# A graph network kernel's first edge layer: finer node ranges per column, sums in seven slots a block, a small PSUM bank in two halves

## The chip, the cores and the metric

The kernel runs on one core of a Trainium2 chip. The metric is the device time of one execution in microseconds. The kernel has TensorE (PE; its weight loads are listed apart as PEld), VectorE (DVE), ScalarE (ACT), GpSimd (POOL) and SyncE (SP), which fetch their own instruction streams and meet at semaphores. DMA queues are fed by SP, ACT and POOL.

## What is computed

The reference has four stages over 6250 nodes with 256 features: a message passing layer over 106250 edges, a graph attention layer that chooses among four experts, a second message passing layer, and a second mixture of experts. The change touches the first one only:

```python
h = jnp.concatenate([x[row], edge_attr], axis=1)      # x: layer norm of the nodes
h = jax.nn.relu(h @ W1 + b1)
agg = jax.ops.segment_sum(h, col, num_segments=N_NODES)
cnt = jax.ops.segment_sum(jnp.ones((h.shape[0],), h.dtype), col, num_segments=N_NODES)
agg = agg / jnp.maximum(cnt, 1.0)[:, None]
out = jnp.concatenate([x, agg], axis=1)
return jax.nn.relu(out @ W2 + b2)                     # added to the nodes
```

The edges come sorted by their target node.

## The kernel before

**Blocks and groups.** The nodes are cut into 49 blocks of 128 (the last one has 106). The edges that end in a block lie in one window of 18 columns of 128 edges. A column index is written as a range `k` of three columns (six ranges) and a place `t` in it. A group is the work of 6 columns, the ranges `g` and `g + 3`; three groups make a block, and the stage runs over 147 groups. The product with the node part of `W1` is made beforehand and lies in memory as `y_dram`.

**One turn of the loop.** For group q the loop writes, engine by engine in an order that `Ordered.pin` keeps:

- `join(q-1)`: DVE adds the gathered rows to the products of the edge features (L1518), ACT applies the relu (L1519). The rows lie in a ring of four buffers `h`.
- `hidden(q, 0)`, `hidden(q, 2)`, `hidden(q, 4)`: PE multiplies the turned edge features `et` by `w1b` into `ph` (L1115), eight matmul records in each of the three. An instruction in f32 stands as two records in the trace.
- `add_up(q-2)`: PE sums the rows by node (L1541), with a 0/1 matrix `eq` as weights. Since the edges are sorted, a range reaches only some of the four quarters (32 nodes) of the block, which `QUARTERS` lists. For each column and quarter there is one matmul on a 128 by 32 tile of the array. In groups 0, 1 and 2 of a block these are 12, 12 and 9 matmuls; in the last block all are full 128 by 128 ones (L1533).
- `load_sources(q+2)`: POOL gathers six columns of rows of `y_dram` by index, one indirect DMA for each (L1128). They may overwrite the ring buffer that `add_up(q-2)` read.
- `turn(q+1)`: DVE turns the next edge features (L1500, tile `et`); `equal(q)`: DVE makes `eq` (L1225), with three buffers `eq`, and one buffer `eq4` for the last block.
- `load_attr(q+4)`: SP and ACT issue the edge features' loads (L1410).

**Work in between.** Three times a turn `steps` moves small jobs on by one step: a sort for the attention layer (DVE), the index windows of later blocks (`load_windows`, with two PE transposes and a count), and `end_of(w)`, the end of a block: division by the count, a transpose (L1109), the product with `W2`, layer norm, another transpose, and a product with `wgx`. A job waits between its hops by `yield`. All of these share one PSUM tile `pt` (pool `p1`, one buffer): who asks for it next waits until its last reader is done. The sort ends in `sorted_edges`, which transposes five pieces, copies each to `lt` (two buffers, L1335) and writes it to memory (L1336).

After the stage the first experts' products (L1115 with `ph<-b_all,w`) and the attention layer follow; they take over the PSUM of `ph`.

Of the kernel before, what the change touches and what calls it, by code (L numbers as in the profile page):

```python
# [1 line left out]

# [19 lines left out]
def spread(n):  # L22

    cuts = [n] if n % 16 == 0 else [n // 16 * 16, n]
    return list(zip([0, *cuts[:-1]], cuts))


class Ordered:
# [840 lines left out]
def kernel(ctx: ExitStack, tc: tile.TileContext, a: dict, out: bass.AP):  # L869
# [32 lines left out]
    NR = CW // NT  # L902
    Q = P // 4
    QUARTERS = ((0, 1), (0, 2), (1, 3), (1, 4), (2, 4), (3, 4))
    H, X = a["L0_ffn_att_src"].shape
    HX = H * X
    GW = HX + 2 * H
# [36 lines left out]
    with ExitStack() as fast:  # L944
# [188 lines left out]
        def load_windows(b, pool):  # L1133

            sl = slice(b * TB, (b + 1) * TB)
            n = TB * CW

            def flat3(v):
                return v.rearrange("p w a t -> p w (a t)")

            raw = {k: wix.tile([P, P], I32, name=f"raw_{k}") for k in ("src", "dst")}
            for w in range(b * TB, (b + 1) * TB):
                at, r = (w - b * TB) * CW, start_of(w)
                for k, v in raw.items():
                    rows = a[k][bass.ds(r, WE)].rearrange("(j p) -> j p", p=P)
                    SY.dma_start(v[at : at + CW, :], rows)  # L1146
            for _ in range(3):
                yield

            def turned(k):  # L1150

                pt = pool.tile([P, D], F32, name="pt")[:, 0:n]
                TE.transpose(pt, whole[k][0:n, :], ident[0:n, 0:n])
                return pt

            whole = {}
            for k, v in raw.items():
                whole[k] = v.bitcast(F32)
                V.tensor_copy(whole[k][0:n, :], v[0:n, :])
            yield  # L1160
            pt = turned("src")
            g = wix.tile([P, n], F32, name="ix_g")
            V.tensor_scalar(g, pt, 0.0, float(N), op0=OP.is_lt, op1=OP.mult)
            V.tensor_add(g, g, pt)
            V.tensor_scalar(
                src1[:, sl, :, :].rearrange("p w a t -> p (w a t)"), g, 0.0, float(N - 1),
                op0=OP.max, op1=OP.min,
            )
            yield
            V.scalar_tensor_tensor(  # L1170
                flat3(dst1[:, sl, :, :]), turned("dst").rearrange("p (w k) -> p w k", k=CW),
                float(-b * TB * P), base.unsqueeze(2).to_broadcast([P, TB, CW]),
                op0=OP.add, op1=OP.subtract,
            )
            yield
            inside = wix.tile([P, TB, NR, NT], F32, name="inside")
            d = dst1[:, sl, :, :]
            V.tensor_scalar(flat3(inside), flat3(d), 0.0, None, op0=OP.is_ge)
            V.scalar_tensor_tensor(
                flat3(inside), flat3(d), P - 0.5, flat3(inside), op0=OP.is_lt, op1=OP.mult  # L1180
            )

            n = TB - (b == NB - 1)
            for k, (lo, hi) in enumerate(QUARTERS):
                for limit, op in ((lo * Q - 0.5, OP.is_gt), (hi * Q - 0.5, OP.is_lt)):
                    if 0 < limit < P - 1:
                        V.scalar_tensor_tensor(
                            inside[:, :n, k, :], d[:, :n, k, :], limit, inside[:, :n, k, :],
                            op0=op, op1=OP.mult,
                        )  # L1190
            if n < TB:
                V.scalar_tensor_tensor(
                    inside[:, n, :, :], d[:, n, :, :], LAST - 0.5, inside[:, n, :, :],
                    op0=OP.is_lt, op1=OP.mult,
                )
            V.tensor_reduce(good[:, b : b + 1], flat3(inside), axis=AX.XY, op=OP.add)
# [14 lines left out]
        def equal(pool, w, q):  # L1211


            total = NT * Q * sum(hi - lo for lo, hi in (quarters(w, q), quarters(w, q + NG)))
            if w < T - 1:
                eq = pool.tile([P, EQ], F32, name="eq", bufs=3)
            else:
                eq = pool.tile([P, total], F32, name="eq4", bufs=1)
            found, at = {}, 0
            for k in (q, q + NG):  # L1220
                lo, hi = quarters(w, k)
                n = (hi - lo) * Q
                found[k] = eq[:, at : at + NT * n].rearrange("p (t n) -> p t n", n=n)
                at += NT * n
                V.tensor_tensor(  # L1225
                    found[k], lane[:, None, lo * Q : hi * Q].to_broadcast([P, NT, n]),
                    dst1[:, w, k, :].unsqueeze(2).to_broadcast([P, NT, n]), op=OP.is_equal,
                )
            return found
# [88 lines left out]
        def sorted_edges(pst, wk):  # L1318
# [10 lines left out]
                V.tensor_scalar(some, some, -1.0, 127.0, op0=OP.mult, op1=OP.add)  # L1329
                V.tensor_copy(v, some)  # L1330
            for c in range(KA // P):
                pt = pst.tile([P, 4, P], F32, name="pt")
                TE.transpose(pt[:, 0, :], some[:, c * P : (c + 1) * P], ident)
                lt = wk.tile([P, P], BF16, name="lt")
                SC.activation(lt, pt[:, 0, :], AF.Copy)  # L1335
                SC.dma_start(low_dram[c * P : (c + 1) * P, :], lt)  # L1336
            V.tensor_reduce(good2[:, 1:2], good3[:, :, 0], axis=AX.X, op=OP.add)
# [17 lines left out]
        with ExitStack() as layer:  # L1355
# [40 lines left out]
                return both  # L1396

            V.memset(gtab[:, :, HX : HX + H], 1.0)
            groups1 = [(w, g) for w in range(T) for g in range(NG)]

            def load_attr(q):

# [66 lines left out]
            with (  # L1469
# [1 line left out]
                tc.tile_pool(name="y0", bufs=1) as wy,  # L1471
                tc.tile_pool(name="ph1", bufs=2, space=PSUM) as psh,
                tc.tile_pool(name="pe1", bufs=1, space=PSUM) as pse,
                tc.tile_pool(name="p1", bufs=1, space=PSUM) as psm,
            ):

                ring = [wy.tile([P, G1, HS], F32, name=f"h{i}") for i in range(4)]
                for h in ring:
                    V.memset(h[:, :, D:WS], 1.0)
                equals, et, ph, sums = {}, {}, {}, {}  # L1480

                last_of = [
                    max(k % NG for k, (lo, hi) in enumerate(QUARTERS) if lo <= b < hi)
                    for b in range(4)
                ]
                NQ1 = len(groups1)

                def rows_of(q):
                    return ring[q % len(ring)]

                def load_sources(q):

                    w, g = groups1[q]
                    for j, (k, t) in enumerate(chunk(g)):
                        gather(rows_of(q)[:, j, 0:D], y_dram, src1[:, w, k, t : t + 1])

                def turn(q):

# [22 lines left out]

                def add_up(q):

                    w, g = groups1[q]
                    if g == 0:
                        sums[w] = pse.tile([P, WS], F32, name="pe")
                    h, eq = rows_of(q), equals.pop(q)

                    for j in reversed(range(NT)):
                        for i, k in ((1, g + NG), (0, g)):  # L1530
                            lo, hi = quarters(w, k)
                            if hi - lo == 4:
                                TE.matmul(  # L1533
                                    sums[w], eq[k][:, j, :], h[:, i * NT + j, 0:WS],
                                    start=g == 0 and j == NT - 1 and i == 1,
                                    stop=g == NG - 1 and j == 0 and i == 0,
                                )
                                continue
                            for b in range(lo, hi):
                                at = slice((b - lo) * Q, (b - lo + 1) * Q)  # L1540
                                TE.matmul(  # L1541
                                    sums[w][b * Q : (b + 1) * Q, :], eq[k][:, j, at],
                                    h[:, i * NT + j, 0:WS], start=g == 0 and j == NT - 1,
                                    stop=g == last_of[b] and j == 0,
                                )

                def end_of(w):

# [3 lines left out]
                    V.reciprocal(rc, rc)  # L1552
                    ag = wk.tile([P, D], F32, name="o")
                    SC.activation(ag, pe[:, 0:D], AF.Copy, scale=rc)
                    yield
                    yield
                    gt = wk.tile([P, D], F32, name="o")
                    transposed(psm, gt, ag)
                    yield
                    yield  # L1560
                    pm = psm.tile([P, D], F32, name="pt")
                    both = (b_all[:, w, 0:P], b_all[:, w, P:D], gt[:, 0:P], gt[:, P:D])
                    mm(pm, lambda c: both[c], lambda c: w2[:, c, :], 4)
# [16 lines left out]
                    V.scalar_tensor_tensor(off, mv[:, 0:1], -1.0, rs, op0=OP.mult, op1=OP.mult)  # L1580
                    xn = wk.tile([P, D], F32, name="o")
                    SC.activation(xn, x_all[:, w, :], AF.Identity, bias=off, scale=rs)
                    yield
                    yield
                    transposed(psm, b_all[:, w, :], xn)
                    yield
                    yield
                    pg = psm.tile([P, D], F32, name="pt")
                    mm(
                        pg[:, 0:GW], lambda c: b_all[:, w, c * P : (c + 1) * P],  # L1590
# [35 lines left out]
                                some.remove(n)  # L1626

                for q in range(3):
                    load_sources(q)
                turn(0)  # L1630
                ordered = Ordered(tc)
                for q in range(NQ1 + 2):
# [5 lines left out]
                    if q >= 2:  # L1638
                        add_up(q - 2)
                        if (q - 2) % NG == NG - 1:  # L1640
                            work.append(end_of((q - 2) // NG))
                    if 3 <= q + 2 < NQ1:
                        load_sources(q + 2)
                    if q + 1 < NQ1:
                        turn(q + 1)
                    if q < NQ1:
# [1012 lines left out]
```

## Time and profile before

| | |
|---|---|
| median of 4 runs | 3422.54 us (3417.98 to 3426.49) |
| profiled execution | 3417.23 us, its span 3415.3 us |
| mean granted TensorE clock | 0.904 |
| PE, PEld busy | 3169.7 us (93%), 2533.0 us (74%) |
| DVE, ACT, POOL busy | 2155.8 us (63%), 1127.0 us (33%), 2248.2 us (66%) |
| first and last gather of the stage start | 93.8 us, 1233.6 us |
| records of the sums L1541 | 3168 |

The profile is one execution. Its times count from the first instruction. "Idle before" is what an engine stood still just before the instructions of a row, and behind it stand those whose end released it. Busy shares over the whole span mix stages with different limits, so the stage of the change has to be read by itself.

### The profile page before, as it was taken

The page shows a single profiled execution, that of the slowest core. Times are in us where ns is not written, and L with a number is a line of the kernel's source. Part 1 is how long each engine was busy: PE and PEld are TensorE (multiplying, and loading weights), DVE is VectorE, ACT ScalarE, POOL GpSimd, SP SyncE. Part 2 cuts the span into 40 slices and gives each one's busy share as a digit, 9 for nine tenths or more (in the row PEclk, how much of TensorE's full clock was granted, in tenths as well). Part 3 has the DMA queues.
Part 4 walks back from the last instruction along what each step waited for, and adds up shares of the span by engine and source line. Part 5 has one row for each costly group of instructions (what it writes and reads, how often), then busy time and mean ns, then how long its engine had stood idle before and what let it go on. Part 6 is the DMA issues. An engine that isn't in the chain of part 4 may idle for free.

```text
span 3415.3 us, 57220 instructions
## 1 busy us (share of the span) xinstructions
PE 3169.7 (93%) x18509; PEld 2533.0 (74%) x18509; DVE 2155.8 (63%) x5685; ACT 1127.0 (33%) x2014; POOL 2248.2 (66%) x2364
## 2 busy tenths in 40 slices
PE   7899999999999989999999999995689988989898
PEld 5677777777777777888888888883556666666677
DVE  5677787767766767877575858775234444445464
ACT  5122222222222224345545455661012212212134
POOL 0677777777777736766555556625777777777773
PEclk9999999999999999999999999996566677677797
DMA  6999999999999943334343434443112222222221
GB/s 195 198 211 205 203 202 205 201 197 208 203 209 207 206 111 105 98 83 137 83 124 97 133 85 126 114 97 88 53 53 60 59 59 60 59 59 66 59 63 37
DMA packets 698912, 428.56 MB, mean 125 GB/s; under 512 B 531272, under 2 KB 640315, under 8 KB 698604
## 3 DMA queue, kind: packets, MB, share of 16 engines
q0 software_dynamic: 89408, 178.08, 23.0%
q1 hardware_dynamic: 365948, 187.21, 21.0%
q10 hardware_dynamic: 243248, 59.52, 9.6%
q8 instruction: 150, 2.46, 0.3%
q14 instruction: 158, 1.29, 0.1%
HBM read 382.05 MB, written 42.49 MB: 124 GB/s over the span
## 4 chain that ended last, share of the span: by engine, by line
PE 64%; POOL 14%; DMA 9%; issue 7%; DVE 3%; ACT 1%; SPq 1%; ACTq 0%; POOLq 0%; DVEq 0%
PE ph L1115 31%; POOL hg L1128 13%; PE py L1115 11%; PE po L1884 6%; PE pe L1541 5%; DMA hg<-hp_dram,src 5%; PE pt L1115 4%; PE pe L2524 2%; DMA rb<-low_dram 2%; PE pa L1821 1%; POOL h L1128 1%; DMA ea<-in_edge_attr_dram 1%; PE pt L1109 1%; PE pm L1115 1%; SPq L1146 0%
## 5 line engine op out<-in xcount | busy, mean ns | idle before, releaser
L1128 POOL DMA_INDIRECT h<-y_dram,src x882 | 844.3, 957 | 388.9 <-issue 263.1
L1128 POOL DMA_INDIRECT hg<-hp_dram,src x831 | 786.7, 947 | 267.7 <-issue 223.9
L1128 POOL DMA_INDIRECT sg<-gat_dram,src x640 | 612.3, 957 | 352.2 <-issue 161.5
L1115 PE MATMUL ph<-w1b,et 128*128 128x256 f32 x3528 | 823.5, 385 | 11.5 <-DVE et L1500 10.0
L1115 PEld LDWEIGHTS ph<-w1b,et 128*128 128x128 f32 x3528 | 655.7, 190 | 154.1 <-issue 70.3
L2524 PE MATMUL pe<-eq,hg 128*128 128x96 f32 (+15 forms) x2036 | 435.1, 350 | 151.3 <-DMA hg<-hp_dram,src 129.1
L2524 PEld LDWEIGHTS pe<-eq,hg 128*128 128x128 f32 x2036 | 382.4, 257 | 256.4 <-issue 98.5
L1519 ACT ACTIVATE h<-h 128x1536 f32<-128x1536 f32 x147 | 218.2, 1485 | 586.6 <-DMA h<-y_dram,src 218.8
L1518 DVE TENSOR_TENSOR h<-ph,h 128x1536 f32<-128x1536 f32 x147 | 258.3, 1757 | 228.4 <-PE ph L1115 202.2
L2503 DVE TENSOR_SCALAR eq<-px,dst,ew 128x96 f32<-128x96 f32 x831 | 261.6, 368 | 219.6 <-PE pe L2524 131.5
L1115 PE MATMUL py<-w,hh 128*128 128x256 f32 x1568 | 385.4, 386 | 4.9 <-ACT hh L1720 4.5
L1115 PE MATMUL ph<-b_all,w 128*128 128x256 f32 (+1 forms) x1600 | 386.7, 381 | 2.9 <-issue 2.8
L1115 PEld LDWEIGHTS py<-w,hh 128*128 128x128 f32 x1568 | 290.4, 192 | 41.5 <-ACT hh L1720 6.7
L1115 PEld LDWEIGHTS ph<-b_all,w 128*128 128x128 f32 x1600 | 291.2, 191 | 36.1 <-issue 3.2
L1500 DVE STREAM_TRANSPOSE et<-ea 128x1536 f32<-128x1536 f32 x147 | 260.9, 1775 | 15.4 <-DMA ea<-in_edge_attr_dram 9.3
L1720 ACT ACTIVATE hh<-ph,b 128x256 f32<-128x256 f32 (+1 forms) x400 | 166.2, 467 | 288.5 <-PE ph L1115 280.8
L1884 PE MATMUL po<-pp,B 128*128 128x240 f32 (+10 forms) x1280 | 252.1, 337 | 2.1 <-DVE acc L1890 2.0
L1884 PEld LDWEIGHTS po<-pp,B 128*128 128x128 f32 x1280 | 215.6, 190 | 14.2 <-DVE acc L1890 2.8
L1541 PE MATMUL pe<-h,eq 128*32 128x257 f32 x3168 | 216.8, 384 | 0.0
L1863 DVE TENSOR_TENSOR pp<-px,A 128x960 f32<-128x960 f32 (+10 forms) x160 | 155.9, 974 | 3.9 <-PE po L1884 3.5
L1541 PEld LDWEIGHTS pe<-h,eq 128*32 128x32 f32 x3168 | 95.9, 109 | 83.5 <-issue 30.5
L1720 ACT ACT_TABLE_LOAD x98 | 125.7, 1283 | 49.8 <-PE ph L1115 48.4
(339 smaller groups left out, 3800.7 us busy)
## 6 DMA issues: line engine op xcount, KB each, us to landing
ea<-in_edge_attr_dram SPq DMA_DIRECT2D x588, 96.0 KB
ea<-in_edge_attr_dram ACTq DMA_DIRECT2D x588, 96.0 KB
y<-y SPq DMA_DIRECT2D x196, 128.0 KB
w<-in_L_ffn_W_dram SPq DMA_DIRECT2D x48, 512.0 KB
y<-ys SPq DMA_DIRECT2D x96, 256.0 KB
rb<-low_dram SPq DMA_DIRECT2D x80, 256.0 KB
h<-y_dram,src POOLq DMA_INDIRECT x882
hg<-hp_dram,src POOLq DMA_INDIRECT x831
```

What stands on the lines that cost most here:

```text
L1109: TE.transpose(pt[:, c, :], src[:, c * P : (c + 1) * P], ident)
L1115: TE.matmul(dst, lhs(c), rhs(c), start=c == 0, stop=c == n - 1)
L1128: GP.indirect_dma_start(out=dst, out_offset=None, in_=table[0:NP, :], in_offset=IndirectOffsetOnAxis(ap=idx, axis=0),)
L1500: V.transpose(et[q].rearrange("p c m k -> p m c k"), ahead.pop(q).rearrange("p i m (c k) -> p (i m) c k", c=2),)
L1518: V.tensor_add(h, ph.pop(q), h)
L1519: SC.activation(h, h, AF.Relu)
L1541: TE.matmul(sums[w][b * Q : (b + 1) * Q, :], eq[k][:, j, at], h[:, i * NT + j, 0:WS], start=g == 0 and j == NT - 1, stop=g == last_of[b] a ...
L1720: SC.activation(hidden[u][:, f, :n, :], ph[:, f - f0, :n, :], AF.Gelu, bias=b1[:, e, f : f + 1],)
L1863: V.tensor_tensor(pps[g, half][:, :, 0:n, :], pay[:, js, :].unsqueeze(2).to_broadcast([P, HG, n, HV]), near[g][:, js, 0:n].unsqueeze(3).to ...
L1884: TE.matmul(po.rearrange("p b v -> p (b v)"), B[:, j, :], pp[:, j, 0:n, :].rearrange("p b v -> p (b v)"), start=half == 0 and j == 0, stop ...
L2503: V.tensor_scalar(equals[k][:, j, :], lanes[:, 0:NW], dst_of[:, t : t + 1], ew[:, t : t + 1], op0=OP.is_equal, op1=OP.mult,)
L2524: TE.matmul(sums[b][:, lo - t0 * P : hi - t0 * P], hg[:, j, :], eq[:, j, lo - n0 : hi - n0], start=False, stop=after >= (t0 + n) * P,)
```

## The change

It has six parts.

- **Ranges for each column.** `RANGES` gives each of the 18 columns its own range of quarters, instead of one for three columns. There are 26 pairs of column and quarter in a block instead of 33. `load_windows` tests whether the edges keep to these ranges, in six instructions over several columns instead of ten over three.
- **Slots.** `planned()` writes the 26 matmuls as slots of up to four, one for each quarter, and gives the three groups of a block 2, 2 and 3 slots. The groups run in the order 2, 0, 1 (`TURNS`). A column that finds no slot in its own group is summed in the next one; only the columns at places 2 and 5 of a group (`LATE1`) may be.
- **Gathers.** The columns of `LATE1` are loaded one turn later, ahead of the next group's other four.
- **`eq`.** Four buffers instead of three; the last block takes two of them for a group instead of the one of its own.
- **The bank.** `pt` becomes one tile of two halves, handed out in turn by `Halves`.
- **Hops.** `end_of` waits three steps instead of two at four places; `lt` has one buffer instead of two.

```diff
+    TURNS, SLOTS = (2, 0, 1), (2, 2, 3)
+    RANGES = (((0, 1), 3), ((0, 2), 2), ((1, 2), 2), ((1, 3), 3), ((2, 3), 1), ((2, 4), 3), ((3, 4), 4))
+    reach = [r for r, n in RANGES for _ in range(n)]
...
+class Halves:
+    def __init__(self, pool, width):
+        self.width, self.last = width, 1
+        self.bank = pool.tile([P, 2, width], F32, name="pt")
+    def tile(self, shape, dtype, name):
...
+            self.last = 1 - self.last
+            v = self.bank[:, self.last, 0:n]
...
-            if w < T - 1:
-                eq = pool.tile([P, EQ], F32, name="eq", bufs=3)
-            else:
-                eq = pool.tile([P, total], F32, name="eq4", bufs=1)
...
+                if eq is None or w == T - 1:
+                    eq, at = pool.tile([P, EQ], F32, name="eq", bufs=4), 0
...
-                lt = wk.tile([P, P], BF16, name="lt")
+                lt = wk.tile([P, P], BF16, name="lt", bufs=1)
...
-            groups1 = [(w, g) for w in range(T) for g in range(NG)]
+            groups1 = [(w, g) for w in range(T) for g in TURNS]
...
+                    for i, g in enumerate(TURNS):
+                        for j, (k, t) in enumerate(chunk(g)):
+                            for b in range(*reach[k * NT + t]):
+                                left[b].append((i, j, k, t))
+                        for n in range(SLOTS[i]):
+                            for b in range(4):
+                                if left[b]:
+                                    plan.append((i, b, *left[b].pop(0)))
...
+                LATE1 = (NT - 1, 2 * NT - 1)
+                EARLY1 = tuple(j for j in range(G1) if j not in LATE1)
...
+                    for i, b, own, j, k, t, start, stop in plan:
+                        if i == turn:
+                            of = q - turn + own
+                            lo = QUARTERS[k][0]
+                            TE.matmul(
+                                sums[w][b * Q : (b + 1) * Q, :],
+                                equals[of][k][:, t, (b - lo) * Q : (b - lo + 1) * Q],
+                                rows_of(of)[:, j, 0:WS], start=start, stop=stop,
+                            )
...
-                    yield
-                    yield
+                    for _ in range(3):
+                        yield
...
+                    if 3 <= q + 1 < NQ1:
+                        load_sources(q + 1, LATE1)
                     if 3 <= q + 2 < NQ1:
-                        load_sources(q + 2)
+                        load_sources(q + 2, EARLY1)
```

## The prediction

> **What bounds the kernel now.** The change lies in the first edge layer, so I cut the span by windows of time first. The two lines below hold the quiet part of the stage (only sums, products and block ends) and the part in which index windows are also made.
>
> ```profile
> 861.00:1230.20 369.20, 369.20 (x2467) 287.76 (x2466) 259.17 (x433) 105.44 (x176) 275.94 (x289) 1.00 0.94 204
> 176.00:860.00 684.00, 671.83 (x4476) 520.25 (x4471) 518.04 (x1005) 189.90 (x319) 501.81 (x525) 1.00 1.03 204
> ```
>
> After the window and its length stand PE, PEld, DVE, ACT and POOL in us, then the granted clock, the DMA share and GB/s. PE is without a gap in the quiet part and lacks 12 us in the other; the clock is full. The chain that ended last says the same, and gives the prices (start, us, what):
>
> ```profile
> 1199.64 1.73 PE ph L1115 x8
> 1201.36 1.44 PE pe L1541 x24
> 1202.80 5.38 PE ph L1115 x24
> 1208.18 0.22 PE pt L1109 x2
> 1208.40 1.43 PE pe L1541 x18
> 1209.83 3.65 PE ph L1115 x16
> ...
> 1231.44 1.43 PE pe L1541 x18
> ```
>
> Everything on it is PE. From 1208.40 to 1231.44 is one block of three groups: 23.05 us. Eight records of 256 columns take 1.73 us, 0.216 each. A sum of 18 records (9 matmuls) takes as long as one of 24 (12 matmuls): four quarters run side by side, and what counts is the number of rounds, not of matmuls. Three slots of two rounds (f32 makes two records) are six rounds.
>
> The second resource to look at is POOL, in the answer for the gathers' line:
>
> ```profile
> L1128 POOL DMA_INDIRECT h<-y_dram,src x882: 940/947/1374, 93.8 to 1233.6; - x177
> L1128 POOLq EVENT_SEMAPHORE  x147: 42/4259/9199, 87.3 to 1220.2; - x147
> ```
>
> In the timeline one gather follows the other with 0.30 us between. From 199.17 to 233.15, 27 steps without a wait take 33.98 us, 1.2585 each; 18 of them are 22.65 us, and a block takes 23.05. So POOL is just behind PE, with 0.4 us a block in hand. That the joins wait for PE and hardly for gathers stands in the costliest groups:
>
> ```profile
> L1518 DVE TENSOR_TENSOR h<-ph,h 128x1536 f32<-128x1536 f32 x147 | 258.3, 1757 | 228.4 <-PE ph L1115 202.2 <-DMA h<-y_dram,src 20.6 <-PE pt L1115 4.7
> ```
>
> Last, the end of the stage. DVE's waits from 1230 to 1262, and the timeline at the copies of `lt`:
>
> ```profile
> DVE eq L1225 <- PE pe L1533: 12.4, 2, 7.1
> ```
> ```profile
> 1263.93 0.28 ACT L1335 ACTIVATE lt<-pt 128x128 bf16<-128x128 f32 x1 [0.87 <-DMA low_dram<-lt]
> 1264.24 0.33 ACTq L1336 DMA_DIRECT2D low_dram<-lt  x1
> ```
>
> The single `eq4` holds DVE until the sums of the group before are done, and the join behind it waits too. The last product of the stage ends at 1245.0, the last join starts at 1251.67, and the experts' first products start at 1253.5, when that join gives their PSUM free.
>
> **The change part by part.**
>
> *Slots (PE).* A block goes from nine slots to 2+2+3. Each slot less is two rounds of 0.216: 0.432 us; two a block are 0.864, and over 48 blocks 41.5 us (the last block keeps its full matmuls). From 33 to 26 matmuls nothing more comes. The step in and out of the 32-wide form is paid once a group as before. A block on PE is then 23.05 - 0.86 = 22.19 us.
>
> *Gathers (POOL).* Their number and bytes stay. With PE at 22.19 and POOL at 22.65 a block, POOL becomes the bound. Its line: first start at 93.8, and 881 steps. At 1.2585 the last one starts at 1202.5 instead of 1233.6, 31.1 us sooner. Bounds: at 0.947 + 0.305 = 1.252 it is 1196.8; at the mean of 957 ns, 1.262, it is 1205.6; should the gathers stretch as much again as the gap of mean over median, 1.272, it is 1214.4. I take the unblocked row. On top, POOL now runs ahead: the gathers of group 144 end 11.0 us before its join (1218.54 to 1229.54). Where POOL was the late one, early in the stage, it was 4.6 us at group 3 (123.7 to 128.3) and 3.15 us at group 6 (146.28 to 149.43). The difference to their mean, 3.9, is 7.1 us; it is taken up once and is a gain too. The transfers' rate must rise by 2%, from 204 GB/s to 208; the window from 800 to 900 us has 208 already.
>
> *Late columns.* Two of six gathers move to the next turn, ahead of the other four, so POOL's stream keeps its order of groups. All six wait for `add_up(q-2)` as before. For the late pair a turn is lost: they end some 2.5 us after that sum and must land before a join some 10 us later; landing at group 6 took less than 3.15. Free.
>
> *Semaphores on POOL.* In the built program the gathers hold 716 semaphore instructions, 573 more. Upper bound: 42 ns each on POOL's line, 24 us. Lower: 0, since today's 147 stand ahead of the first gather of a group and the gap there, unblocked, is the same 0.30 us. That row is the same engine and instruction; I take 0.
>
> *`eq`.* With four buffers the last two `equal` no longer wait for the sums of the group before. The last join moves from 1251.67 towards the end of its product at 1245.0: up to 6.7 us. In the other groups a DVE wait on `eq` does not show (the 12.4 us above are all). Free.
>
> *The bank in halves, and the hops.* PE's waits for `pt` between 90 and 1255 us (rows of `pt` on ACT and DVE) sum to about 14 us. At most these go, and in the part with the index windows they would let PE run nearer to POOL; but POOL is the later one there, so I count 0; the bounds are 0 and what rival 4 makes of it. The steps of `end_of` are the same instructions, and in the quiet part no wait hangs on them. At the end of the stage the block's chain is run without turns in between, so longer hops cost nothing there.
>
> *`lt` with one buffer.* Each of five copies waits for the write of the one before: 0.28 + 0.33 + about 1.45 (the chain has such writes at 1.45 and 1.48) is 2.06 us instead of about 0.93 (four steps from 1262.06 to 1265.77). ACT is free 4.2 to 4.5 us later. Behind it stand the experts' first activations, for which PE waits; but before that PE has the last block's sums (4.3 us). I take +2, bounds 0 and +4.5.
>
> *Window test, DVE.* Six instructions for ten, a few tenths a window: nothing.
>
> [...] The row for the halves is the 14 us of waits, counted at 0. The Trainium skill, "PSUM — Partial Sum Buffer", section "PSUM bank collisions raise a hardware error", asks to guard PSUM by bank and quadrant, not by address; guarded like that the halves would bring nothing, which leaves the sum as it is. The row for the gathers has a mean of 957 ns over a median of 947, so other work costs them 10 ns each, 9 us in all; the same DVE work in 2 to 4% less time adds under 1 us. [...]
>
> **The sum**, against the profiled execution. Last join by POOL: 1202.5 + 0.95 + 3.9 = 1207.4. By PE: 1245.0 - 41.5 = 1203.5. The later counts, 1207.4; it was 1251.67, so -44.3. With `lt` +2: -42.3. What follows is the same list of work on PE, apart from a few instructions at the seam, so it moves as a whole. 3417.23 - 42.3 = 3374.9. The median of the runs lies 5.3 above the profiled run; I keep that: 3380.
>
> **The rivals.**
>
> 1. *POOL pays for the semaphores or stretches.* For it: POOL has little in hand, and nearly each gather now waits for PE too. Against: today's unblocked gap with a semaphore. At 24 us the last join is at 1231, the gain 18: 3404.
> 2. *Slower: the clock.* Once PE waits for gathers it has gaps. Where PE was busy 57 to 73 of 100 us (2300 to 2500), the granted clock was 0.62 and 0.52. For it: that stage also waits for gathers. Against: from 176 to 860 PE lacks 1.8% and the clock is 1.00, and here it would lack 0.46 of 22.65 us, 2%. A us at half clock costs PE half a us, and PE has 4 us in hand (1203.5 against 1207.4): with x us at half clock the time is 3380 + x/2 - 4. From x = 93 it is no gain, from 107 of the 1110 us it is slower by over 0.2%; at 120 it is 3436.
> 3. *The change doesn't bring the rounds.* If the new order of quarters doesn't run side by side, the rounds stay nine slots' worth, and only the end of the stage gains: -6.7 + 2, 3418. Against: the 9 and the 12 matmuls of today take the same 1.43 us.
> 4. *POOL does not bind.* If the gathers step at 1.252 and the waits for `pt` go, the last join is at 1201 and `lt` is hidden: -51, 3372.
>
> **How the numbers follow.** The forecast with its bounds (steps of 1.252 to 1.272, `lt` 0 to 4.5) gives 3372 to 3395, chance 0.65. Rival 4: 0.12. Rival 1: 0.11, 3390 to 3410. Rival 3: 0.04. Rival 2: 0.08, two thirds of it above the old time. Eight in ten: from 3367 (rival 4 less 4 to 5 us, by which the runs scatter about their median) to 3402. A measurement can tell 0.2%, 6.8 us, from no change: faster 0.90, same 0.04, slower 0.06.
>
> **What the profile after would show.** The sums at 1.0 us for the first two groups of a block and 1.43 for the third; 2496 records instead of 3168. A block at 22.6 to 22.7 us in the quiet part, PE with gaps of some tenths, POOL's steps at 1.26 with next to no waits, joins that wait for gathers and no longer for PE. The last gather near 1202. No wait of `eq` for L1533. Wrong would be: steps of POOL above 1.29, sums of 1.43 in all groups, a granted clock under 1 in the stage, or a new wait of PE for `h` or `pt` longer than today's.

## The result: 0.2% slower; the slots' time came back as waits for `pt`

The changed kernel takes 3432.18 us (median of 39 runs, 3417.08 to 3443.91), the kernel before 3423.82 us beside it (62 runs). The ratio is 1.0023, 95% interval 1.0017 to 1.0029. The profiled execution after has a span of 3425.6 us and took 3427.48; before, 3415.3 and 3417.23. The forecast was 3380 us, the range 3367 to 3402.

The slots did what they were meant to do. The group of the sums on the page, and in the timeline the third sum of a block and the three of the next, the last of them cut short by the window's end at 900 us (start, us, engine, line, instruction):

```profile
L1583 PE MATMUL pe<-h,eq 128*32 128x257 f32 x2496 | 175.4, 385 | 0.0
```
```profile
876.93 1.51 PE L1583 MATMUL pe<-h,eq 128*32 128x257 f32 x24
...
883.97 1.07 PE L1583 MATMUL pe<-h,eq 128*32 128x257 f32 x12
...
890.92 1.07 PE L1583 MATMUL pe<-h,eq 128*32 128x257 f32 x16
...
899.03 1.29 PE L1583 MATMUL pe<-h,eq 128*32 128x257 f32 x20
```

2496 records stand where 3168 stood, two-slot sums take 1.07 us and three-slot ones 1.51, the sums' busy time falls from 216.8 to 175.4 us, and the block from 876.93 to 899.03 takes 22.10 us; it was 23.05. Now the same windows of time as before the change, for the part with index windows and for the quiet part:

```profile
176.00:860.00 684.00, 645.04 (x4003) 505.62 (x4003) 509.45 (x987) 183.39 (x312) 489.91 (x512) 0.98 0.95 199
861.00:1230.20 369.20, 364.04 (x2280) 285.22 (x2279) 263.61 (x438) 105.51 (x179) 279.56 (x292) 1.00 1.12 209
```

In the first part PE lacks 39 of 684 us; it lacked 12. From 90 us to the join of group 144 (1229.5 before, 1238.3 after) PE was busy for 1116.5 us before and 1087.9 after, and stood still for 23.0 and 60.4: 28.6 us less work and 37.4 us more standing make the join 8.8 us later. A second pair of profiles (`before_again`, `after_again`) has 37.0 us more standing too, but 38.5 us less work, and there the join comes 1.5 us sooner. So the standing takes back what the slots save, to within a few us. Where the 0.2% come from is not shown: the stage's last join starts 2.9 us later in the first pair and 5.6 us sooner in the second, and behind it the spans go on for 7 and 9 us longer, which is inside the scatter of such stretches (2164 to 2178 us over the profiles of the table below).

PE's waits from 90 to 1250 us say for what (engine, tile and line, what ended the wait: us in all, times, longest):

```profile
PE pt L1136 <- ACT a_dst L1637: 26.1, 8, 8.9
PE pt L1130 <- ACT b_all L1131: 20.3, 9, 8.0
PE ph L1136 <- DVE et L1545: 10.3, 2, 5.8
PE ph L1136 <- DVE rc L1593: 2.1, 4, 0.7
PE pt L1130 <- ACT o L1624: 1.4, 1, 1.4
```

The first two rows are 46.4 us in 17 waits; all waits for `pt` were about 14 us before. L1136 after is L1115 before (products), L1130 is L1109 (transposes), L1564 is L1519 (relu).

The longest one in the timeline. ACTq and SPq are the issues of DMAs; the bracket is the engine's idle time and what ended it:

```profile
623.33 0.28 SPq L1167 DMA_DIRECT2D raw_dst<-in_dst_dram  x1
623.49 0.52 PE L1136 MATMUL pt<-wgx,b_all 128*128 128x24 f32 x4
...
627.66 6.17 ACTq L1434 DMA_DIRECT2D ea<-in_edge_attr_dram  x4
...
631.29 0.28 SPq L1167 DMA_DIRECT2D raw_dst<-in_dst_dram  x1
...
634.10 1.48 ACT L1564 ACTIVATE h<-h 128x1536 f32<-128x1536 f32 x1 [13.42 <-DMA h<-y_dram,src]
635.49 0.17 ACT L1635 ACTIVATE gtab<-pt 128x16 f32<-128x16 f32 x1
...
635.61 0.17 ACT L1637 ACTIVATE a_dst<-pt 128x4 f32<-128x4 f32 x1
635.83 1.36 PEld L1136 LDWEIGHTS pt<-w,b_all 128*128 128x128 f32 x4 [9.30 <-ACT a_dst L1637]
635.83 2.08 PE L1136 MATMUL pt<-w,b_all 128*128 128x256 f32 x4 [8.89 <-ACT a_dst L1637]
```

To be read from the end. PE wants to write the product with `W2` (L1136, `pt<-w,b_all`) and waits 8.89 us for the copy of `a_dst`. That copy reads the *other* product, `pt<-wgx,b_all`, which PE had made at 623.49 into the other half: the halves don't free PE from it, since the wait is one for the whole tile. The copy is late because ACT works in order: ahead of it stands the relu at 634.10, and ahead of that the issue of four edge feature loads from 627.66 to 633.83, while SP issues the raw indices of an index window (619.10 to 631.29). The join that the relu needed had begun at 621.97 already, and ACT had done nothing since 620.67. What held it are waits for semaphores at the loads, not the issues; ACT's instructions at the loads' line from 618 to 636 us (count, shortest/median/longest ns, first and last start):

```profile
L1434 ACTq DMA_DIRECT2D ea<-in_edge_attr_dram x4: 323/341/370, 627.7 to 633.5; - x4
L1434 ACTq EVENT_SEMAPHORE  x2: 38/3390/6742, 620.7 to 620.8; - x2
```

An issue takes 0.34 us; ahead of the first stands a wait of 6.74. In the trace's records each of the four loads uses the semaphore of a `raw_src` load that SP issued before it, waits for that semaphore, and goes out just behind that load's landing: landings at 627.53, 629.09, 630.39 and 633.43, issues at 627.66, 629.11, 630.42 and 633.45. So ACT is held until SP's index loads have landed. In this trace and in those of the kernel before and of `even_c` it is so in all six index windows: 24 of ACT's 588 loads follow a `raw_src` load on their semaphore, all 24 by 0.02 to 0.23 us after its landing.

Where a use of `pt` stands in the block's nine steps (three a turn) follows from the code. With hops of two, a block's end uses `pt` at steps 2 (transpose of `ag`), 4 (product with `W2`), 8 (transpose of `xn`) and 10 (product with `wgx`, step 1 of the next block); with hops of three at 3, 6, 11 and 14, which are 3, 6, 2 and 5 of the nine. So with three, two pairs of uses in a block lie one step apart (2 and 3, 5 and 6), both from a turn's first call of `steps` to its second. Only a sum and eight records of `ph` lie between them on PE, while on ACT the copy between them stands behind the loads issued at the end of the turn before and behind the new turn's relu. With two, one pair is as close (1 and 2), from the third call to the first of the next turn, and its copy is issued ahead of the loads.

Theory H (hold and hops) says that the stall needs both: uses one step apart with a copy of ACT between them, and ACT held by its loads. Rival G: POOL is the bound anyway, and the waits for `pt` only stand where waits for gathers would stand. Rival A: ACT is held whatever the hops are, and the waits move elsewhere.

### The profile page after: what moved, and what is told of

The parts are those of the page before. It is cut to its first block, busy times and chain, and to the rows that moved or that the text cites. A ratio compares the mean times of both kernels' runs of the same rounds, so it can differ in the third digit from the quotient of the medians.

```text
span 3425.6 us, 56495 instructions
## 1 busy us (share of the span) xinstructions
PE 3129.6 (91%) x17837; PEld 2510.1 (73%) x17837; DVE 2156.9 (63%) x5678; ACT 1120.5 (33%) x2013; POOL 2248.7 (66%) x2364
## 4 chain that ended last, share of the span: by engine, by line
PE 53%; DMA 16%; POOL 13%; issue 7%; DVE 6%; ACT 2%; SPq 2%; ACTq 0%; DVEq 0%; POOLq 0%
PE ph L1136 25%; POOL hg L1149 12%; PE py L1136 11%; DMA hg<-hp_dram,src 6%; DMA ea<-in_edge_attr_dram 6%; PE po L1928 5%; PE pt L1136 3%; PE pe L1583 3%; PE pe L2568 2%; DMA h<-y_dram,src 2%; DMA rb<-low_dram 2%; DVE et L1545 1%; PE pa L1865 1%; PE pt L1130 1%; DVE x_all L2109 1%
## 5 line engine op out<-in xcount | busy, mean ns | idle before, releaser
L1136 PE MATMUL ph<-w1b,et 128*128 128x256 f32 x3528 | 830.8, 387 | 12.4 <-DVE et L1545 10.3
L1136 PEld LDWEIGHTS ph<-w1b,et 128*128 128x128 f32 x3528 | 660.7, 192 | 159.1 <-issue 71.3
L1564 ACT ACTIVATE h<-h 128x1536 f32<-128x1536 f32 x147 | 218.3, 1485 | 545.3 <-DMA ea<-in_edge_attr_dram 274.1
L1136 PE MATMUL py<-w,hh 128*128 128x256 f32 x1568 | 384.6, 385 | 5.9 <-ACT hh L1764 5.1
L1136 PE MATMUL ph<-b_all,w 128*128 128x256 f32 (+1 forms) x1600 | 385.3, 380 | 0.3 <-DVE h L1563 0.3
L1136 PEld LDWEIGHTS py<-w,hh 128*128 128x128 f32 x1568 | 289.5, 191 | 42.8 <-ACT hh L1764 7.7
L1136 PEld LDWEIGHTS ph<-b_all,w 128*128 128x128 f32 x1600 | 290.2, 190 | 32.9 <-DVE h L1563 0.7
L1583 PE MATMUL pe<-h,eq 128*32 128x257 f32 x2496 | 175.4, 385 | 0.0
L1136 PE MATMUL py<-ew,g 65*128 65x256 f32 x392 | 132.5, 465 | 0.3 <-ACT g L2488 0.2
```

Source lines behind the costliest of these rows:

```text
L1136: TE.matmul(dst, lhs(c), rhs(c), start=c == 0, stop=c == n - 1)
L1564: SC.activation(h, h, AF.Relu)
L1583: TE.matmul(sums[w][b * Q : (b + 1) * Q, :], equals[of][k][:, t, (b - lo) * Q : (b - lo + 1) * Q], rows_of(of)[:, j, 0:WS], start=start, s ...
```

## The experiments where the kernel before takes 3427 to 3429 us

### Spacing alone, and hold alone

Hops of two again (`hops2_c`), an even spacing (`even_c`: uses at 0, 2, 4 and 6 of the nine), the halves and hops alone on the kernel before (`before_halves_hops3_c`), and ACT's loads given to SP, which takes the reading of their start address from ACT too (`sp_loads_c`):

```diff
 hops2_c, at all four places in end_of
-                    for _ in range(3):
+                    for _ in range(2):
 even_c, at the first, second and fourth place; the third keeps range(3)
-                    for _ in range(3):
+                    for _ in range(2):
...
-                    for _ in range(3):
+                    for _ in range(2):
...
-                    for _ in range(3):
+                    for _ in range(6):
 before_halves_hops3_c, on the kernel before: class Halves, psm = Halves(pends, D), and
-                    yield
-                    yield
+                    for _ in range(3):
+                        yield
 sp_loads_c
-                r = start_of(w, mybir.EngineType.Activation)
+                r = start_of(w)
...
-                        (SY if c < 2 else SC).dma_start(
+                        SY.dma_start(
```

hops2_c:

> The changed kernel with hops of two steps, now where the kernel before takes 3427 us and the changed one 3434. Theory H (the hops): 3385 to 3400 us, PE's waits for `pt` under 20 us. Rival G (the gathers are the bound anyway): 3420 to 3435. Rival A (ACT is held by its issue of loads whatever the hops, and the waits move to other uses of `pt`): 3410 to 3425.

even_c:

> The changed kernel with hops of 2, 2, 3 and 6 steps (uses of `pt` at 0, 2, 4 and 6 of a block's nine steps), where the kernel before takes 3427 us. Theory H: waits for `pt` of 5 to 15 us and 3378 to 3398 us, at or under hops of two. Rival A: 3410 to 3430.

before_halves_hops3_c:

> The kernel before with only the halves and the hops of three steps, where the kernel before takes 3427 us. Theory H: 3445 to 3475 us, waits of PE for `pt` of 40 us or more. Rival G: 3420 to 3432. Rival S (the waits need the shorter blocks of the new slots): 3427 to 3442.

sp_loads_c:

> The changed kernel with hops of three steps and all edge feature loads issued by SP, where the kernel before takes 3427 us. If ACT's hold in the issue is the second half of the cause: waits of PE for `pt` under 25 us, 3395 to 3415 us. If the copy is late in any case: waits of 40 us or more, 3420 to 3437. Late edge features would show as waits of DVE's transposition for its loads.

The changed kernel and the kernel before were run once more (`after_again`, `before_again`; what was expected of them stands with the first set of runs below), and the changed kernel gave 3434.47 us there, beside 3426.79 for the kernel before, ratio 1.0029 (1.0017 to 1.0042).

| kernel | us | ratio to before, 95% interval |
|---|---|---|
| hops2_c | 3408.92 | 0.9944 (0.9928 to 0.9960) |
| even_c | 3395.66 | 0.9899 (0.9880 to 0.9918) |
| sp_loads_c | 3395.02 | 0.9904 (0.9886 to 0.9921) |
| before_halves_hops3_c | 3455.43 | 1.0079 (1.0061 to 1.0097) |

Against the changed kernel (3434.47) that is -25.6, -38.8 and -39.5 us. On the kernel before, halves and hops of three cost 26.7 us. Rival G falls: the gathers let the kernel go 39 us faster. Rival A falls as a whole, since ACT's loads are the same in `even_c`; but `hops2_c` came out above the 3385 to 3400 of theory H, at 3408.92, so hops of two keep a part of the stall. Its largest row is a wait for `xn` (L1624), which ACT makes behind the same loads, so a part of the waits did move, as rival A has it. PE's waits from 90 to 1250 us, first `hops2_c`, then `sp_loads_c`, then `before_halves_hops3_c`:

```profile
PE pt L1130 <- ACT o L1624: 13.8, 3, 6.4
PE ph L1136 <- DVE et L1545: 9.6, 2, 5.7
PE pt L1136 <- ACT o L1131: 5.6, 5, 2.1
```
```profile
PE pt L1136 <- ACT a_dst L1637: 7.7, 12, 2.1
PE pt L1130 <- ACT b_all L1131: 7.3, 6, 2.3
```
```profile
PE pt L1127 <- ACT b_all L1128: 15.9, 5, 6.5
PE pt L1133 <- ACT a_dst L1614: 12.2, 3, 4.4
```

With ACT free the same two rows as in the changed kernel remain (uses one step apart), but shrink from 46.4 us to 15.0, the longest from 8.9 to 2.3. In the kernel before the halves and hops bring the same two rows, 28.1 us, under the 40 that were expected. They stand in place of 14.1 us of other waits for `pt`, so the loss of 26.7 is not these waits alone: up to group 144's join PE stands 16.5 us more and is busy 10.9 us more than in the profile of the kernel before (table below).

All waits for `pt` up to 1250 us sum to 47.8 us in the changed kernel, 32.2 in `hops2_c` (expected under 20), 26.9 in `even_c` (5 to 15) and 23.6 in `sp_loads_c` (under 25). They fell, but two of the three by less than expected. A part lies behind the joins of the last groups; up to group 144's join they are 47.8, 26.0, 16.7 and 14.5. In `even_c` the largest row is `PE pt L1136 <- ACT o L1131: 11.9, 8, 3.7`, the product with `W2` waiting for the copy of the transpose two steps before.

In `even_c` ACT is held as well, but in the index window for the same block PE does not wait for it:

```profile
607.48 4.38 ACTq L1434 DMA_DIRECT2D ea<-in_edge_attr_dram  x4
...
610.03 0.52 PE L1136 MATMUL pt<-wgx,b_all 128*128 128x24 f32 x4
...
612.14 1.48 ACT L1564 ACTIVATE h<-h 128x1536 f32<-128x1536 f32 x1 [11.17 <-DMA raw_src<-in_src_dram]
...
613.74 0.17 ACT L1637 ACTIVATE a_dst<-pt 128x4 f32<-128x4 f32 x1
...
617.29 0.38 PE L1130 MATMUL pt<-ident,o 128*128 128x128 f32 x2
```

ACT again stands idle for 11.17 us before the relu, the copy of `a_dst` ends at 613.91, and PE's next use of `pt` is at 617.29, without a bracket: it did not wait.

### Both, and the parts alone

`even_sp` has the even spacing and SP's loads; `before_sp` is the kernel before with SP's loads; `hops2_onebank_c` has hops of two and `pt` from a pool of one buffer; `hops2_onebank_sp` has SP's loads on top of that.

```diff
 hops2_onebank_c, hops2_onebank_sp
-                tc.tile_pool(name="p1", bufs=1, space=PSUM) as pends,
+                tc.tile_pool(name="p1", bufs=1, space=PSUM) as psm,
...
-                psm = Halves(pends, D)
```

even_sp:

> The changed kernel with the even spacing (hops of 2, 2, 3 and 6) and all edge feature loads issued by SP: both halves of the cause taken away, and the candidate for a version that beats both. Each alone gave 3395 us. If both take away the same waits for `pt` (theory H: spacing and hold are two conditions of one stall, and either suffices), the two together give little more: 3382 to 3396 us, and the bound is POOL, with the last gather near 1205. If they were two separate losses, they add up: 3355 to 3370.

before_sp:

> The kernel before with all edge feature loads issued by SP, nothing else. Theory H: it has only some 14 us of waits for `pt` and PE is the bound, so taking away ACT's hold brings little: 3412 to 3428 us. Then the slots' share without the hold is the distance from here to the changed kernel with SP's loads (3395), 17 to 33 us, less what POOL binds. Rival: the hold costs every version alike and SP's loads gain by themselves what they gained in the changed kernel, 39 us: 3385 to 3395.

hops2_onebank_c:

> The changed kernel with hops of two steps and `pt` from a pool of one buffer, no halves, where the kernel before takes 3427 us. Theory H: the halves decouple nothing, so within 0.2% of the kernel with halves and two steps (3409): 3402 to 3416 us. Rival: the halves let PE go on while ACT copies; then 5 to 20 us slower, 3414 to 3429.

hops2_onebank_sp:

> As the one before, with all edge feature loads issued by SP: of the change only the slots, the gathers and `eq` are left, and ACT is not held. Theory H: with no hold the spacing hardly matters, so about the same as the even spacing with SP's loads, 3382 to 3398 us. If the spacing costs something without the hold too, it is slower than that by 5 to 15 us.

| kernel | us | ratio to before, 95% interval |
|---|---|---|
| even_sp | 3388.10 | 0.9882 (0.9861 to 0.9902) |
| before_sp | 3423.07 | 0.9986 (0.9975 to 0.9997) |
| hops2_onebank_c | 3408.40 | 0.9941 (0.9923 to 0.9959) |
| hops2_onebank_sp | 3395.29 | 0.9899 (0.9878 to 0.9919) |

Both together take 46.4 us off the changed kernel's 3434.47, where each alone took 39: it is mostly one stall with two conditions, and taking either away takes most of it. In the kernel before the loads' engine is worth 6 us at most, about what a measurement can tell, so the hold costs where something waits for it. Measured with SP's loads in both, the change is worth 28 us (`hops2_onebank_sp` against `before_sp`) to 35 (`even_sp`). The halves bring nothing that shows: 3408.92 with them, 3408.40 without. By the code, hops of three may need them in this order: with those hops an index window's transpose can ask for `pt` before the reader of the product with `W2` is issued. Hops of three on a pool of one buffer were not tried. Without the hold, the difference between even spacing with halves and two-step spacing without is 7.2 us, which is about the size that a measurement can tell; whether the spacing costs anything on its own is open. `even_sp` is the fastest version of the case.

### What bounds the kernel when the stall is gone

POOL's rows for the gathers (count: shortest, median, longest ns, first and last start), of the changed kernel, `even_c` and `even_sp`:

```profile
L1149 POOL DMA_INDIRECT h<-y_dram,src x882: 940/946/1652, 94.8 to 1247.1; - x177
```
```profile
L1149 POOL DMA_INDIRECT h<-y_dram,src x882: 940/946/1469, 95.1 to 1216.7; - x177
```
```profile
L1149 POOL DMA_INDIRECT h<-y_dram,src x882: 942/947/1734, 95.0 to 1209.9; - x177
```

From the records of these rows I take the mean step from start to start where the gap to the next gather is under 0.33 us, and for the longer gaps what they are above 0.325:

| | first gather | step without wait | POOL's waits | last gather | last join starts | PE busy, idle from 90 us to group 144's join |
|---|---|---|---|---|---|---|
| before | 93.8 | 1.2625 | 27.1 | 1233.6 | 1251.7 | 1116.5, 23.0 |
| before_again | 97.7 | 1.2670 | 26.9 | 1241.2 | 1259.2 | 1124.4, 22.7 |
| forecast | 93.8 | 1.2585 | 0 | 1202.5 | 1207.4 | |
| after | 94.8 | 1.2641 | 38.5 | 1247.1 | 1254.6 | 1087.9, 60.4 |
| after_again | 94.6 | 1.2666 | 37.0 | 1247.5 | 1253.6 | 1085.9, 59.7 |
| before_halves_hops3_c | 95.9 | 1.2656 | 47.7 | 1261.0 | 1280.3 | 1127.4, 39.5 |
| hops2_c | 94.7 | 1.2652 | 20.8 | 1230.4 | 1236.4 | 1088.4, 39.6 |
| even_c | 95.1 | 1.2666 | 5.7 | 1216.7 | 1225.0 | 1083.7, 31.0 |
| sp_loads_c | 95.6 | 1.2643 | 0 | 1209.4 | 1216.5 | 1080.6, 28.4 |
| even_sp | 95.0 | 1.2656 | 0 | 1209.9 | 1216.6 | 1081.1, 26.4 |

The measured lines add up to within 0.5 us, `before_halves_hops3_c` to 2.5: 95.0 + 881 x 1.2656 = 1210.0 for `even_sp`. Where the stall is gone, POOL runs from the first gather to the last without a wait, as the forecast had it. The joins of `even_sp` wait for gathers now (the group of the joins: busy, mean ns, idle before and what ended it), where they waited for PE before:

```profile
L1563 DVE TENSOR_TENSOR h<-ph,h 128x1536 f32<-128x1536 f32 x147 | 258.1, 1756 | 235.8 <-DMA h<-y_dram,src 154.3 <-PE ph L1136 34.1 <-issue 14.8
```

In the changed kernel the ring of four buffers couples the two: while PE stands, no sum frees a buffer and POOL stands too (in its trace sums end 65.0 us of POOL's idle time, 92 times, with some 0.30 us in each that POOL stands idle anyway). At 1.264 a gather a block takes POOL 22.75 us against PE's 22.10, so POOL has nothing in hand and can't make it up.

## The first set of runs, where everything took 4170 us and more

Two sets of four kernels ran where the kernel before itself took 4173.45 and then 4170.78 us, 22% above its time elsewhere. They are chips 0 and 10 on record; the runs above come from chips 3, 6 and 13.

hops2 and hops2_b (hops of two):

> The changed kernel with its four hops of three steps set back to two, as before; all else of the change stays. Theory H (the hops): the changed profile shows PE waiting 26.1 us for a_dst's copy and 20.3 us for b_all's copy out of `pt`, some 45 us that the kernel before did not have, because with three steps two uses of `pt` on PE lie one step apart with ACT's copy between them. With two steps these waits fall back to about 14 us in all, and the slots' saving shows: 3385 to 3400 us, PE's waits for pt under 20 us. Rival G (the gathers): POOL is the bound anyway, and the waits for pt only stand where waits for gathers would stand; then the time stays at 3420 to 3435 and the joins' waits for gathers grow by what the pt waits lose. Rival A (ACT held): ACT is held by the issue of its edge feature loads whatever the hops are, so the waits move to other uses of `pt`: 3410 to 3425.

> The kernel with hops of two steps again: in its first run the kernel before itself took 4173 us instead of 3423, the loads and gathers came late everywhere and the joins waited for them, so that run says nothing on waits for `pt` where the loads are in time. On a chip where the kernel before takes about 3423 us, theory H (the hops) expects 3385 to 3400 us and PE's waits for `pt` under 20 us; rival G (the gathers are the bound anyway) 3420 to 3435; rival A (ACT is held whatever the hops) 3410 to 3425.

hops2_onebank:

> As the kernel with hops of two steps, and the two halves taken out too: `pt` comes from a pool of one buffer, as before. Theory H says that the halves decouple nothing (in the changed kernel each use of `pt` waits for the copy of the other half): within 0.2% of the kernel with halves and two steps, 3385 to 3400 us. Rival: the halves do let PE go on while ACT copies; then this one has 5 to 15 us more of waits for `pt` and is as much slower.

before_halves_hops3 and before_halves_hops3_b:

> The kernel before with only the halves and the hops of three steps; quarters, slots, gathers and `eq` as before. Theory H: the hops cost some 45 us of waits, of which a part was in the gaps that PE had anyway: 3445 to 3475 us, and waits of PE for `pt` of 40 us or more. Rival G: PE was the bound before and the hops cost nothing there: 3415 to 3430. Rival S (the waits need the shorter blocks of the new slots): 3425 to 3440.

> The kernel before with only the halves and the hops of three steps, again for a chip where the kernel before takes about 3423 us. Theory H: 3445 to 3475 us, waits of PE for `pt` of 40 us or more. Rival G: 3415 to 3430. Rival S (the waits need the shorter blocks of the new slots): 3425 to 3440.

sp_loads and sp_loads_b:

> The changed kernel, hops of three steps kept, with all edge feature loads issued by SP; ACT issues none of them, so it is not held in the issue. Theory H with ACT's hold as the second half of the cause: ACT's copies come in time, the waits of PE for `pt` fall from 46 to under 25 us, and the time is 3395 to 3415. If the hold does not matter (the copy stands behind the relu in any case), the waits stay at 40 us or more and the time at 3420 to 3435. A cost on the other side: SP also issues the index loads, and edge features that come late would show as waits of DVE's transposition L1545 for its loads.

> The changed kernel with hops of three steps and all edge feature loads issued by SP, again for a chip where the kernel before takes about 3423 us. If ACT's hold in the issue is the second half of the cause, the waits of PE for `pt` fall from 46 to under 25 us and the time is 3395 to 3415; if the copy is late in any case, the waits stay at 40 us or more and the time at 3420 to 3435. Late edge features would show as waits of DVE's transposition for its loads.

even:

> The changed kernel with hops of 2, 2, 3 and 6 steps, which puts the four uses of `pt` by a block's end at steps 0, 2, 4 and 6 of the nine of a block, so that no two are one step apart. Theory H: PE's waits for `pt` fall to 5 to 15 us, and the time is at or under that with two steps everywhere: 3378 to 3398 us. If the waits come from ACT being held, not from the spacing, it stays at 3410 to 3430.

| kernel | us | ratio to before, 95% interval |
|---|---|---|
| hops2, hops2_b | 4271.57, 4258.25 | 1.0228 (1.0183 to 1.0272), 1.0201 (1.0167 to 1.0236) |
| hops2_onebank | 4268.26 | 1.0219 (1.0173 to 1.0264) |
| before_halves_hops3, \_b | 4191.76, 4185.93 | 1.0029 (0.9996 to 1.0063), 1.0036 (1.0010 to 1.0061) |
| sp_loads, sp_loads_b | 4195.78, 4195.14 | 1.0053 (1.0026 to 1.0080), 1.0045 (1.0024 to 1.0066) |
| even | 4180.09 | 1.0023 (0.9998 to 1.0048) |

None of the expectations on the time held. PEld's waits from 300 to 1200 us, first of `even`, then of the same kernel as `even_c`:

```profile
PEld ph L1136 <- issue: 97.5, 173, 1.3
PEld pe L1583 <- issue: 76.7, 168, 1.3
```
```profile
PEld ph L1136 <- issue: 49.5, 121, 0.4
PEld pe L1583 <- issue: 25.6, 86, 0.3
```

There PE stood still between single instructions, up to 1.3 us each time, for nothing that the profile shows, and the first join of a block came 14 to 23 us after the last of its gathers had ended on POOL, against 3 to 13 in `even_c`. The packets of the gathers were no slower (220 ns in the median there, 274 in `even_c`); the mean granted clock of the profiled runs was 0.85 to 0.87, against 0.90. What held the engines is open, and with it why hops of two are 2% slower there and the even spacing is not; neither a profile of the kernel before nor a run of the changed kernel exists from there. That the halves bring nothing shows there too (4271.57 with, 4268.26 without). `after_again` and `before_again` were to settle it and ran where the kernel before took 3427 us:

after_again:

> The changed kernel itself, beside the kernel before, on the chip of the experiments. There the kernel before took 4171 us, PE stood still for `issue` between single instructions and the joins waited longer; the ratio of 1.0023 was measured where it took 3424. Theory H in its plain form (the changed kernel loses 46 us to the spacing of three steps, wherever it runs) expects the changed kernel to be slower than the one with even spacing (4180) by some 30 to 45 us: 4205 to 4230. If PE is not the bound here, the waits for `pt` cost nothing: 4175 to 4195, as the two kernels with hops of three steps.

before_again:

> The kernel before, for its profile on the chip of the experiments: 4150 to 4200 us if that chip is as it was, 3420 if not. If it is as it was, its first stage shows where the 750 us more lie: PE's idle time for `issue`, the granted clock and the landing of the gathers against the profile at 3417 us.

They took 3434.47 and 3429.81 us (the second a single run), so the ranges given for a kernel before at 4171 don't apply. The waits of `after_again` repeat the two rows of the changed kernel, 23.8 us in 11 and 21.6 in 10.

## Why the prediction was wrong, by its steps

- **Slots: right.** 0.95 us a block where PE waits for nothing (23.05 to 22.10), against 0.86 worked out; 41.4 us of the sums' busy time in all, against 41.5.
- **Gathers, POOL as the bound: right once the stall is gone, not in the changed kernel.** There POOL waits 38.5 us instead of none. The term was also too small: I took the step from 27 gathers without a wait (1.2585); over all of them in the same trace it is 1.2625, in the second profile of the kernel before 1.2670, and in `even_sp` 1.2656. The difference from 1.2585 is 6.3 us over 881 steps and explains most of why `even_sp` stands at 3388 and not at 3380.
- **Semaphores on POOL: right at 0.** With these instructions the changed kernel and its variants in the table step at 1.2641 to 1.2666, and without them the kernel before at 1.2625 and 1.2670 in its two profiles. A cost does not show beside that scatter of 4 us over the stage; the 24 of the upper bound would.
- **Bank and hops: the step that failed.** Of the 52.6 us by which the profiled run missed its 3374.9, 47.2 lie at the last join (1254.6 instead of 1207.4) and 5 behind it. I wrote that the steps of `end_of` are the same instructions and "in the quiet part no wait hangs on them", and set 0, with bounds of 0 and a gain. I looked for waits that the edit takes away, and only in the quiet part. I didn't lay the uses of `pt` beside each other in the new order, nor ask what stands on ACT between two of them in the part with index windows. There ACT stood idle for up to 13.42 us ahead of a relu with the copy behind it, and the slots' saving was gone: PE waited 47.8 us for `pt` instead of 14.1, and POOL 38.5 us where the forecast had none (27.1 before). Spacing the uses evenly alone, and freeing ACT from the loads alone, each brought 39 us back. The trace of before had the same hold, 9.59 us ahead of the relu at 622.16 with its four loads from 616.92; but the next use of `pt` behind it waited 0.66 us only.
- **The rule of the Trainium skill** ("PSUM — Partial Sum Buffer", section "PSUM bank collisions raise a hardware error": guard by bank and quadrant, not by address) was cited for the halves, and the trace agrees: 8.89 us of waiting for a copy of the other half, and 0.5 us between the kernels with hops of two with and without halves. I stopped at "the halves would bring nothing". With closer hops the same rule says that a wait is added.
- **`eq`: right in size.** From group 144's join to the start of the last one it takes 16.3 and 18.0 us after, in the two profiles, instead of 22.1, so 5.8 and 4.1 against up to 6.7; in `even_sp`, where POOL binds, 19.1.
- **`lt`: right in the mechanism.** The five copies step at 1.86 us (7.43 us for four steps) against 2.06 worked out; before, 0.93. PE waits for them 4.6 us instead of 1.9. Behind the last join the spans go on for 2164 and 2169 us before, 2171 and 2178 after, and 2164 to 2178 in all profiles of the table, so whether this cost the 2 us can't be told from the spans.
- **The rivals.** Missing rounds: no. The clock: a small part, which goes with the stalls. From 176 to 860 us the granted clock is 0.98 in both profiles of the changed kernel and in `before_halves_hops3_c`, where PE lacks 27 to 39 of the 684 us, and 1.00 in both of the kernel before, in `sp_loads_c` and in `even_sp`, where it lacks 9 to 12. PE's busy time in the last column of the table differs by 6.8 us between the changed kernel and `even_sp`. The slower case had another mechanism than the one I named. "A new wait of PE for `pt`" stood among what would show the forecast wrong, and had no price.

## What to carry to other kernels

When small steps that share a buffer are moved apart or together, write down the positions of all its uses in one period, and between each two neighbours what stands ahead of the copy on its engine; an in-order engine that also issues loads makes every copy behind them as late as the loads, and here a load was as late as the landing of another engine's load on the same semaphore. Price it in the phase where that engine is held, not in the quiet one. Two halves of one PSUM tile are one buffer as long as the wait covers the whole tile, as it did here.

## What was not expected of the hardware

- ACT's issue of four loads took 4 to 6 us while SP issued 14 small loads (6.17 us above, 4.38 in `even_c`), and ACT had stood idle for 11 to 13 us when its next activation began. That is no slow issue of the chip, since an issue took 0.34 us: the loads of the two engines share semaphores, and ACT waited for the landings of SP's. With all loads on SP the same kernel was 39 us faster, though SP then issues twice as many of the edge feature loads.
- Moving the loads' engine is worth 6 us in the kernel before and 39 in the changed one.
